# Two more steps before the normalizations of a routing batch, and the sigmoids of two batches in one place

## The chip, the core and the metric

The kernel runs on one core of a Trainium2 chip. The metric is device time in microseconds of one execution, given as the median of several runs. A profiled execution comes beside it; all durations below are from that one. Engines are named as in the profile: PE (TensorE), PEld (its weight loads), ACT (ScalarE), DVE (VectorE), POOL (GpSimd), SP (SyncE, which only issues DMAs).

## The reference, cut to what matters

The kernel computes a layer norm, then the sum of the input, a gated linear attention and a mixture of 64 experts, for 4 sequences of 2048 tokens with 256 features.

```python
xn = _layernorm(x)                                   # 8192 tokens x 256
# attention, 8 heads, keys of 128, values of 64, per token:
alpha = sigmoid((xn @ Wg + bg) / 16)                 # the decay of each head
state = alpha * state + k * v
out_t = einsum(q, state)
attn = (out * sigmoid(xn @ Wog)) @ Wo
# experts:
scores = sigmoid(xn @ gate_w.T)                      # 8192 x 64
# 4 of 8 groups by their two best scores + bias, then the 8 best experts of these;
# an expert takes its first 256 tokens
y = (silu(x_e @ w_gate) * (x_e @ w_up)) @ w_down     # added to the token, weighted by its scores
x = x + attn + moe
```

The decay `alpha` and the `scores` both come from one product of a token with 64 + 8 columns, and both go through a sigmoid.

## The kernel before

**Stages.** The tokens pass in 16 routing batches of 512 (`RB`, index `b`) and 32 attention blocks of 256 (index `s`). The attention blocks run one behind another over the whole kernel. Beside the first 16 of them run the fronts and backs of the routing batches, beside the later ones the experts.

**Steps.** The order of the work is written out in `block(s)`. A block has two halves; each takes the output products `od` of the half before, the state's update `dp`, then two projections of keys (`pj` with `wk`), two of queries (`wq`), transposes of keys (`kp`), the output projection (`wo`), values (`wv`) and gates (`wog`), and products of keys and queries (`sp`). Between these parts it calls `step()`, 12 times a block (`STEPS`). A step advances each generator in the list `side` whose start is due to its next `yield True`. Fronts of batches from 3 on start 12 steps apart, one per block: `start_front(b)` is `(b - 2) * STEPS`. `back(b)`, which picks the experts from the scores, starts at step `b * STEPS + 3`; `decays(i)` starts with the last batch of its group (`DGROUPS`: batches 0; 1; 2 and 3; 4 to 7; 8 to 11; 12 to 15).

**A front.** `front(b)` takes the statistics on DVE (L350 to L359); at the next step POOL works out the factors `rstd` and `nb` of the normalization in 14 small operations (L375 to L380) and SP loads the next batch's rows (`load_x`). Then come four steps, each with one ACT normalization of 128 tokens (L396), and after every second of these an ACT cast to fp16 (`x16`, L400) and a POOL subtraction for the low part (L401). The rows go to `xw_d` in DRAM (L404); `turn_tokens` transposes them on PE (`tp`, L340); the transposed tokens go to `xT_d` (L412). Last comes the product `lg` with the routing and decay columns, an addition of the bias on DVE (`zs`, L425), and two sigmoids on ACT: `sg` (L428, for the decays) and `sc` (L430, the scores).

**The decays.** `decays(i)` takes the logarithm of `sg` on ACT (L442), and later exponentials (L460, L462). The blocks use ACT for the high fp16 part of every projection (`split`, L229; DVE makes the low part from it, L230), for exponentials (L956) and for a tanh (L879). Sigmoid, Ln and Exp lie in different ACT tables; where a function is not in the table that is loaded, the compiler puts an `ACT_TABLE_LOAD` before it, which the profile shows under the line of that function.

**Order on an engine.** Each engine runs its instructions in order. A planner at build time chooses that order out of the program's order and its own times (`schedule_with_timeline_sim=True`); `tc.issue_after(x)` tells it to put instructions behind `x`. So an edit in one place can move instructions in others. PSUM tiles of the blocks come from a pool of four (`ps["pj"]`), those of routing and experts from a pool of two (`ps["mo"]`).

Of the kernel before, what the change touches and what calls it, by code (L numbers as in the profile page):

```python
# [13 lines left out]
AF = mybir.ActivationFunctionType  # L14
# [11 lines left out]
E, CAP, I = 64, 256, 128  # L26
# [39 lines left out]
def bc(ap, axis, n):  # L66

    a = ap.unsqueeze(axis)
    shape = list(a.shape)
    shape[axis] = n  # L70
    return a.to_broadcast(shape)
# [3 lines left out]
def gla_moe_kernel(ctx: ExitStack, tc: tile.TileContext, x, Wq, Wk, Wv, Wo, Wg, bg, Wog,  # L75
                   gate_wT, gate_bias, w_gate, w_up, w_down, out):
    nc = tc.nc
# [68 lines left out]
    made = {}  # L146
    WQ, WK, WV, WOG, GATE, WG = range(6)
# [5 lines left out]
    unfit = const.tile([P, 6], F32, name="unfit")  # L153
# [122 lines left out]
    def product(out_, a, b, first=True, last=True):  # L276

        nc.tensor.matmul(out_, lhsT=a[0], rhs=b[0], start=first, stop=False)  # L278
        nc.tensor.matmul(out_, lhsT=a[0], rhs=b[1], start=False, stop=False)  # L279
        return nc.tensor.matmul(out_, lhsT=a[1], rhs=b[0], start=False, stop=last).ins  # L280
# [40 lines left out]
    zs = r1.tile([P, NB, H, RT], F32, name="zs")  # L321
    sg = r1.tile([P, NB, H, RT], F32, name="sg")
    batch = {}

    def load_x(b):
        rows = slice(b * RB, (b + 1) * RB)
        xt = r2.tile([P, RT, D], F32, name="xt")
        src = xf[rows, :].rearrange("(t p) d -> p t d", p=P)
        n = 2 if b == 0 else RT
        for t in range(0, RT, n):  # L330
            nc.sync.dma_start(out=xt[:, t:t + n], in_=src[:, t:t + n])
        batch[b] = {"xt": xt}

    def turn_tokens(x16, xT):
        for t in range(0, RT, 2):
            tp = ps["mo"].tile([P, 2, 2, 2, P], F16, tag="mo", name="tp")
            for t2 in range(2):
                for a in range(2):
                    for c in range(2):
                        nc.tensor.transpose(tp[:, t2, a, c, :], x16[:, t + t2, a, c * P:(c + 1) * P], identh)  # L340
            nc.vector.tensor_copy(xT[:, t:t + 2], tp)

    def front(b):

        rows = slice(b * RB, (b + 1) * RB)
        xt = batch[b].pop("xt")
        st = r2.tile([P, RT, 6], F32, name="st")
        mv = r2.tile([P, RT, 2], F32, name="mv")
        for t in range(RT):
            nc.vector.bn_stats(out=st[:, t, :], in_=xt[:, t, :])  # L350
        for t in range(RT):
            nc.vector.bn_aggr(out=mv[:, t, :], in_=st[:, t, :])

        va = r2.tile([P, RT], F32, name="va")
        nc.vector.tensor_scalar(va, mv[:, :, 1], EPS, XFIT ** -2, ALU.add, ALU.mult)
        yi = r2.tile([P, RT], I32, name="yi")
        nc.vector.tensor_scalar(yi, va.bitcast(I32), 1, None, ALU.logical_shift_right)
        rstd = r2.tile([P, RT], F32, name="rstd")
        nc.vector.tensor_scalar(rstd.bitcast(I32), yi, -1.0, float(0x5f3759df), ALU.mult, ALU.add)  # L359
        yield True  # L360
        nt = r2.tile([P, RT], F32, name="nt")
        nb = r2.tile([P, RT], F32, name="nb")
        x16 = r1.tile([P, RT, 2, D], F16, name="x16")
        flat = x16.rearrange("p t a d -> p t (a d)")
        xT = r2.tile([P, RT, 2, 2, P], F16, name="xT")
        if b < 2:
            for _ in range(3):
                nc.vector.tensor_tensor(nt, rstd, rstd, ALU.mult)
                nc.vector.scalar_tensor_tensor(nt, in0=nt, scalar=-0.5, in1=va, op0=ALU.mult, op1=ALU.mult)
                nc.vector.scalar_tensor_tensor(rstd, in0=nt, scalar=1.5, in1=rstd, op0=ALU.add, op1=ALU.mult)  # L370
            nc.vector.scalar_tensor_tensor(nb, in0=mv[:, :, 0], scalar=-1.0, in1=rstd,
                                           op0=ALU.mult, op1=ALU.mult)
        else:
            for _ in range(3):
                nc.gpsimd.tensor_tensor(nt, rstd, rstd, ALU.mult)  # L375
                nc.gpsimd.tensor_tensor(nt, nt, va, ALU.mult)
                nc.gpsimd.tensor_scalar(nt, nt, -0.5, 1.5, ALU.mult, ALU.add)
                nc.gpsimd.tensor_tensor(rstd, rstd, nt, ALU.mult)
            nc.gpsimd.tensor_tensor(nb, mv[:, :, 0], rstd, ALU.mult)
            nc.gpsimd.tensor_scalar(nb, nb, -1.0, None, ALU.mult)  # L380
        if b < 2:
            for t in range(RT):
                made["hi"] = nc.scalar.activation(x16[:, t, 0, :], xt[:, t, :], AF.Identity,
                                                  bias=nb[:, t:t + 1], scale=rstd[:, t:t + 1]).ins
                xn = t5.tile([P, D], F32, tag="t5", name="xn")
                with tc.issue_after(made["xn"]) if b == 0 and t == 2 else ExitStack():
                    nc.vector.tensor_scalar(xn, xt[:, t, :], rstd[:, t:t + 1], nb[:, t:t + 1], ALU.mult, ALU.add)
                made["xn"] = nc.vector.tensor_tensor(x16[:, t, 1, :], xn, x16[:, t, 0, :], ALU.subtract).ins
        else:
            if b < NB - 1:  # L390
                load_x(b + 1)

            for t in range(RT + 1):
                yield True
                if t < RT:
                    nc.scalar.activation(xt[:, t, :], xt[:, t, :], AF.Identity,  # L396
                                         bias=nb[:, t:t + 1], scale=rstd[:, t:t + 1])
                if t in (2, 4):
                    ts = slice(t - 2, t)
                    nc.scalar.copy(x16[:, ts, 0, :], xt[:, ts])  # L400
                    nc.gpsimd.tensor_tensor(x16[:, ts, 1, :], xt[:, ts], x16[:, ts, 0, :], ALU.subtract)  # L401
        if b < 2:
            turn_tokens(x16, xT)
        made["xw"] = nc.sync.dma_start(out=xw_d[rows, 0:D].rearrange("(t p) d -> p t d", p=P),  # L404
                                       in_=flat.bitcast(F32)).ins
        yield True
        if b >= 2:
            if b > 2:
                yield True
            turn_tokens(x16, xT)  # L410
            yield True
        stored = nc.sync.dma_start(out=xT_d[b], in_=xT)  # L412
        with tc.issue_after(stored.ins):
            nc.sync.dma_start(out=of[rows, :], in_=xf[rows, :])
        batch[b]["xT"] = xT
        if b == 1:
            load_x(2)
        for _ in range(2 if b > 2 else 1):
            yield True
        lg = ps["mo"].tile([P, RT, E + H], F32, tag="mo", name="lg")  # L420
        for t in range(RT):
            for c in range(2):
                made["lg"] = product(lg[:, t, :], (xT[:, t, 0, c, :], xT[:, t, 1, c, :]),
                                     (gwz[:, 0, c, :], gwz[:, 1, c, :]), c == 0, c == 1)
        nc.vector.scalar_tensor_tensor(zs[:, b].rearrange("p h t -> p t h"), in0=lg[:, :, E:E + H],  # L425
                                       scalar=unfit[:, WG:WG + 1], in1=bc(brow, 1, RT),
                                       op0=ALU.mult, op1=ALU.add)
        nc.scalar.activation(sg[:, b], zs[:, b], AF.Sigmoid)  # L428
        sc = r3.tile([P, RT, E], F32, name="sc")
        nc.scalar.activation(sc, lg[:, :, 0:E], AF.Sigmoid, scale=unfit[:, GATE:GATE + 1])  # L430
        batch[b]["sc"] = sc
        yield True

    def decays(gi):
# [361 lines left out]
    side = []  # L796
# [381 lines left out]
    nc.vector.tensor_scalar(brow, brow, 1.0 / GATE_NORM, None, ALU.mult)  # L1178
    squares(WOG, raw["wog"][1][0][1])
    f0 = front(0)  # L1180
    for _ in range(3):
        next(f0)
# [70 lines left out]
    def start_front(b):  # L1253
        return 0 if b < 2 else 8 if b == 2 else (b - 2) * STEPS

    side.append((20, expert_fits(FITS[0])))
    for b in range(NB):
        if b:
            f = front(b)
            side.append((start_front(b), f))  # L1260
            if b == 1:
                with after(made["lo wk"]):
                    next(f)
        side.append((b * STEPS + (3 if b else 5), back(b)))
        for i, (b0, nb_) in enumerate(DGROUPS):
            if i and b0 + nb_ - 1 == b:
                side.append((start_front(b) + (12 if b > 2 else 6), decays(i)))

    unit_l(0, 0, 0)
    unit_a(0, 0, 0)  # L1270
# [54 lines left out]
```

## Time and profile before

| | |
|---|---|
| runs, median (lowest to highest) | 1272.43 us (1270.54 to 1278.66), 3 runs |
| the profiled execution | 1262.07 us |
| its span, first to last instruction | 1260.3 us |
| mean granted PE clock | 0.995 |
| busy: PE, PEld, DVE, ACT, POOL | 1188.0, 1018.4, 981.5, 914.0, 717.0 us |
| ACT table loads | 39, of 1283 ns each |
| normalizations on ACT (L396) | 56, mean 591 ns |

A group's row in the profile reads: line, engine, operation, output<-inputs, shape, count | busy time, mean of one in ns | idle time of the engine just before these instructions, and what ended it. A row of waits reads: who waited <- for what: total us, times, longest us. A row of the timeline reads: start in us, duration, engine, line, operation.

### The profile page before, as it was taken

The numbers are of one execution on the slowest core, as the hardware profiler recorded it, in microseconds if no ns is written. First come the engines' busy times: TensorE is split into PE (matmuls) and PEld (weight loads), VectorE is DVE, ScalarE is ACT, GpSimd is POOL, SyncE is SP. The second block draws the span as 40 slices with busy tenths as digits, with TensorE's granted clock in tenths as the row PEclk, the third lists the DMA queues.
The fourth block names the chain that finished last, engine by engine and source line by source line (L and its number), as shares of the span: only waits on it lengthen the run. The fifth ranks groups of instructions, "written<-read, shape, count | busy, mean of one in ns | idle before, by whom it ended". The sixth has DMA issues, their size and how long they took to land.

```text
span 1260.3 us, 35303 instructions
## 1 busy us (share of the span) xinstructions
PE 1188.0 (94%) x13799; PEld 1018.4 (81%) x13799; DVE 981.5 (78%) x2757; ACT 914.0 (73%) x1664; POOL 717.0 (57%) x899
## 2 busy tenths in 40 slices
PE   7799999999999998999799999999999999999997
PEld 6588777777888777788688888888888888888886
DVE  6988867686787876777778788878787878787864
ACT  5567676676767676666578898878888778778864
POOL 1476657765666566644335675626676757665330
PEclk9999999999999999999999999999999999999999
DMA  7446544535445554432657787768877777666531
GB/s 242 133 126 183 156 136 148 151 94 152 117 131 163 157 143 129 134 100 73 184 144 171 192 207 191 184 154 194 217 194 177 153 181 167 163 146 145 115 68 35
DMA packets 192615, 190.57 MB, mean 151 GB/s; under 512 B 35456, under 2 KB 163328, under 8 KB 191744
## 3 DMA queue, kind: packets, MB, share of 16 engines
q1 hardware_dynamic: 158928, 138.75, 36.2%
q0 software_dynamic: 29712, 45.89, 20.7%
q10 hardware_dynamic: 3808, 3.67, 0.8%
q8 instruction: 108, 1.77, 0.6%
q14 instruction: 59, 0.48, 0.1%
HBM read 141.14 MB, written 58.38 MB: 158 GB/s over the span
## 4 chain that ended last, share of the span: by engine, by line
PE 52%; DVE 19%; ACT 8%; POOL 8%; issue 6%; DMA 6%; SPq 2%; DVEq 0%; POOLq 0%; ACTq 0%
PE pj L278 8%; PE pj L280 8%; PE pj L279 8%; PE od L997 3%; PE od L1003 2%; PE kp L936 2%; DVE qt L912 2%; DVE ql L230 2%; PE xet L694 2%; PE gu L280 2%; PE gu L278 2%; PE gu L279 2%; DVE dc L981 2%; DMA el<-el_d 2%; POOL ol L1042 1%
## 5 line engine op out<-in xcount | busy, mean ns | idle before, releaser
L754 POOL DMA_INDIRECT out_dram<-y,idx x128 | 214.1, 1673 | 158.6 <-ACT y L740 50.8
L672 POOL DMA_INDIRECT xe<-xw_d,idx x128 | 137.5, 1074 | 40.3 <-issue 30.5
L278 PE MATMUL pj<-xs,wq_h 128*128 128x256 f16 x496 | 136.1, 274 | 8.2 <-DVE k L230 6.5
L230 DVE SCALAR_TENSOR_TENSOR k<-pj,k 128x512 f16<-128x512 f32 x128 | 87.0, 684 | 69.2 <-ACT k L229 68.3
L280 PE MATMUL pj<-xs,wq_l 128*128 128x256 f16 x496 | 136.2, 275 | 0.0
L279 PE MATMUL pj<-xs,wq_h 128*128 128x256 f16 x496 | 136.1, 274 | 0.0
L279 PE MATMUL pj<-xs,wk_h 128*128 128x256 f16 x496 | 135.2, 273 | 0.2 <-issue 0.2
L280 PE MATMUL pj<-xs,wk_l 128*128 128x256 f16 x496 | 135.2, 273 | 0.0
L278 PE MATMUL pj<-xs,wk_h 128*128 128x256 f16 x496 | 135.2, 273 | 0.0
L981 DVE TENSOR_TENSOR dc<-sp,dc 128x512 f32<-128x512 f32 x128 | 87.7, 685 | 46.4 <-POOL dc L961 25.5
L997 PE MATMUL od<-dc,v 128*64 128x128 f32 x1024 | 101.3, 279 | 4.5 <-DVE dc L981 4.5
L279 PE MATMUL sp<-ql,k 128*128 128x128 f16 x512 | 96.1, 219 | 7.8 <-DVE ql L230 6.9
L278 PE MATMUL sp<-qh,k 128*128 128x128 f16 x512 | 99.2, 220 | 4.3 <-ACT qh L229 2.2
L229 ACT ACTIVATE k<-pj 128x512 f16<-128x512 f32 x128 | 74.2, 591 | 33.6 <-PE pj L280 26.4
L280 PE MATMUL sp<-qh,k 128*128 128x128 f16 x512 | 96.0, 219 | 0.0
L229 ACT ACTIVATE qh<-pj 128x512 f16<-128x512 f32 x128 | 76.0, 596 | 25.8 <-PE pj L280 21.7
L1003 PE MATMUL od<-qt,state 128*64 128x128 f32 x960 | 94.7, 273 | 0.0
L1041 ACT CAST oh<-oT 128x512 fp32r<-128x512 f32 x64 | 39.6, 618 | 72.4 <-DVE oT L1011 68.6
L230 DVE SCALAR_TENSOR_TENSOR ql<-pj,qh 128x512 f16<-128x512 f32 x128 | 86.8, 679 | 4.4 <-ACT qh L229 4.1
L936 PE MATMUL kp<-identh,k 128*128 128x128 f16 x1024 | 82.5, 220 | 6.2 <-DVE k L230 3.4
L955 ACT ACTIVATE dc<-lp 128x512 f32<-128x512 f32 x128 | 76.3, 596 | 15.8 <-PE lp L951 14.3
L912 DVE SCALAR_TENSOR_TENSOR qt<-pj,el 128x512 f32<-128x512 f32 x128 | 86.8, 679 | 0.7 <-DMA el<-el_d 0.7
(421 smaller groups left out, 4512.0 us busy)
## 6 DMA issues: line engine op xcount, KB each, us to landing
el<-el_d SPq DMA_DIRECT2D x64, 512.0 KB
xw_d<-x SPq DMA_DIRECT2D x16, 512.0 KB
xT_d<-xT SPq DMA_DIRECT2D x16, 512.0 KB
out_dram<-in_L_attn_x_dram SPq DMA_DIRECT2D x16, 512.0 KB
nw<-in_L_ffn_w_gate_dram SPq DMA_DIRECT2D x64, 128.0 KB
nw<-in_L_ffn_w_up_dram SPq DMA_DIRECT2D x64, 128.0 KB
nw<-in_L_ffn_w_down_dram SPq DMA_DIRECT2D x64, 128.0 KB
w<-in_L_ffn_w_gate_dram SPq DMA_DIRECT2D x64, 128.0 KB
```

The costliest lines, as they stand in the source:

```text
L229: return (nc.scalar.activation(hi, t, AF.Copy, scale=scale).ins, nc.vector.scalar_tensor_tensor(lo, in0=t, scalar=scale, in1=hi, op0=ALU.m ...
L230: nc.vector.scalar_tensor_tensor(lo, in0=t, scalar=scale, in1=hi, op0=ALU.mult, op1=ALU.subtract).ins)
L278: nc.tensor.matmul(out_, lhsT=a[0], rhs=b[0], start=first, stop=False)
L279: nc.tensor.matmul(out_, lhsT=a[0], rhs=b[1], start=False, stop=False)
L280: return nc.tensor.matmul(out_, lhsT=a[1], rhs=b[0], start=False, stop=last).ins
L672: in_turn(lambda: nc.gpsimd.indirect_dma_start(out=xe[:, f, :], out_offset=None, in_=xw_d[:, :], in_offset=bass.IndirectOffsetOnAxis(ap=id ...
L754: two = [in_turn(lambda: nc.gpsimd.indirect_dma_start(out=of, out_offset=bass.IndirectOffsetOnAxis(ap=idx[:, e, f:f + 1], axis=0), in_=m[" ...
L912: read = nc.vector.scalar_tensor_tensor(qt, in0=pj, scalar=QFIT, in1=two_heads(el, i), op0=ALU.mult, op1=ALU.mult)
L936: nc.tensor.transpose(kp[:, i, :], k[:, i, :], identh)
L981: anchor.append(nc.vector.tensor_tensor(dc, B["sp"], dc, ALU.mult).ins)
L997: mm = nc.tensor.matmul(od[i * DV:(i + 1) * DV, n, j, :], lhsT=v[:, h0 + 2 * j + i, :], rhs=dc[:, 2 * j + i, :], start=True, stop=first)
L1003: mm = nc.tensor.matmul(od[i * DV:(i + 1) * DV, n, j, :], lhsT=state[half][:, 2 * j + i, :], rhs=qt[:, ck, 2 * j + i, :], start=False, sto ...
```

## The change

- For batches from 3 on, two more steps lie between the POOL factors and the first ACT normalization. All that follows in the front comes two steps later; `decays` starts two steps later as well. `load_x` and `back` keep their steps.
- For the even batches from 2 on, DVE copies the raw products into `sc`, and no sigmoid is taken. With the odd batch behind it, ACT takes `sg` of both batches in one instruction, then the sigmoid of the copied `sc` in place, then that of its own `sc`; `issue_after` keeps the three in this order.

```diff
@@ front(b), batches from 2 on
             if b < NB - 1:
                 load_x(b + 1)
+            if b > 2:
+                for _ in range(2):
+                    yield True
 
             for t in range(RT + 1):
                 yield True
...
-        nc.scalar.activation(sg[:, b], zs[:, b], AF.Sigmoid)
+
         sc = r3.tile([P, RT, E], F32, name="sc")
-        nc.scalar.activation(sc, lg[:, :, 0:E], AF.Sigmoid, scale=unfit[:, GATE:GATE + 1])
         batch[b]["sc"] = sc
+        if b > 1 and b % 2 == 0:
+            nc.vector.tensor_copy(sc, lg[:, :, 0:E])
+        else:
+            b0 = b if b < 2 else b - 1
+            made["sg"] = nc.scalar.activation(sg[:, b0:b + 1].rearrange("p b x y -> p (b x y)"),
+                                              zs[:, b0:b + 1].rearrange("p b x y -> p (b x y)"), AF.Sigmoid).ins
+
+            if b0 < b:
+                with tc.issue_after(made["sg"]):
+                    sc0 = batch[b0]["sc"]
+                    made["sg"] = nc.scalar.activation(sc0, sc0, AF.Sigmoid, scale=unfit[:, GATE:GATE + 1]).ins
+            with tc.issue_after(made["sg"]):
+                nc.scalar.activation(sc, lg[:, :, 0:E], AF.Sigmoid, scale=unfit[:, GATE:GATE + 1])
         yield True
...
-                side.append((start_front(b) + (12 if b > 2 else 6), decays(i)))
+                side.append((start_front(b) + (14 if b > 2 else 6), decays(i)))
```

## The prediction

> **What bounds the kernel now.** I read the page first (engine shares), then the stretches of the run, then TensorE's waits in the routing stretch, then ScalarE's groups there, and last one half-block in order of time.
>
> ```profile
> PE 1188.0 (94%) x13799; PEld 1018.4 (81%) x13799; DVE 981.5 (78%) x2757; ACT 914.0 (73%) x1664; POOL 717.0 (57%) x899
> ```
>
> TensorE (PE) is busy 94% of the span, and no other engine comes near. So the end moves only by what TensorE idles, and the change adds and removes no matmul. The stretches (columns: PE, PEld, DVE, ACT, POOL busy) say where it idles:
>
> ```profile
> 80.00:560.00 480.00, 448.54 (x5381) 378.99 (x5380) 360.04 (x1082) 331.97 (x614) 309.67 (x546) 0.99 0.48 140
> 650.00:1260.00 610.00, 595.96 (x6908) 519.76 (x6905) 489.58 (x1249) 480.57 (x872) 343.21 (x249) 1.00 0.69 161
> ```
>
> From 80 to 560 us the fronts of batches 3 to 15 run beside the attention blocks, and TensorE idles 480 - 448.5 = 31.5 us. The change touches this stretch alone: in the orders of the two built programs TensorE's sequence is the same again once the experts start. **31.5 us (2.5%) is the most that can come of it.** TensorE's own waits there (80 to 600 us; total, times, longest):
>
> ```profile
> PE tp L340 <- ACT x L400: 10.8, 10, 2.7
> PE pj L278 <- DVE k L230: 5.4, 7, 1.2
> PE sp L279 <- DVE ql L230: 4.4, 7, 1.5
> PE kp L936 <- DVE k L230: 2.8, 5, 1.3
> PE kp L936 <- ACT dc L955: 1.9, 2, 1.2
> ```
>
> The first is the change's target: the transposes of a batch's tokens stand still until ScalarE (ACT) has cast the normalized rows. The other four have ScalarE behind them too: VectorE's low parts `k` and `ql` wait for ScalarE's high parts (in this stretch VectorE waits 60.0 us for ScalarE's `k`). So TensorE idles where ScalarE runs late. ScalarE's groups show with what:
>
> ```profile
> L396 ACT ACTIVATE xt<-xt,nb,rstd 128x256 f32<-128x256 f32 x52 | 27.2, 591 | 6.8 <-POOL nb L380 6.8
> L428 ACT ACT_TABLE_LOAD x14 | 18.0, 1283 | 0.2
> L956 ACT ACT_TABLE_LOAD x13 | 16.7, 1283 | 0.2
> L430 ACT ACTIVATE sc<-lg,unfit 128x256 f32<-128x256 f32 x14 | 6.4, 456 | 0.0
> ```
>
> Each front loads the sigmoid table and, soon after, the exp table again. One half-block that starts its `od` products at 190.16:
>
> ```profile
> 194.44 0.62 ACT L1041 CAST oh<-oT 128x512 fp32r<-128x512 f32 x1 [2.60 <-DVE oT L1011]
> 194.96 0.59 ACT L955 ACTIVATE dc<-lp 128x512 f32<-128x512 f32 x1
> 195.57 1.28 ACT L956 ACT_TABLE_LOAD   x1
> 196.86 0.63 ACT L956 ACTIVATE dc<-dc 128x512 f32<-128x512 f32 x1
> 197.40 1.06 ACT L229 ACTIVATE k<-pj 128x512 f16<-128x512 f32 x2
> 198.35 0.60 ACT L955 ACTIVATE dc<-lp 128x512 f32<-128x512 f32 x1
> 198.95 2.08 ACT L396 ACTIVATE xt<-xt,nb,rstd 128x256 f32<-128x256 f32 x4
> ...
> 201.45 0.57 ACT L229 ACTIVATE qh<-pj 128x512 f16<-128x512 f32 x1
> ```
>
> The keys' first projection was done at 194.3, its cast starts at 197.4; a table load and four normalizations stand before `qh`. TensorE idles 0.79 us (for `k`), 0.29 (transposes) and 0.49 (`ql`), 1.6 us in all. Thirteen half-blocks hold normalizations; adding up TensorE's gaps of over 0.25 us in them gives about 27 us, so **2.1 us each**; some 4.5 us lie elsewhere.
>
> **The change, part by part.**
>
> *Two steps more before the normalizations (b > 2).* Nothing is added; normalizations, casts, transposes, the stores of `xw_d` and `xT_d`, logits and decays come two steps later, on SP's queue past the loads of half a block; `load_x(b + 1)` keeps its step. In the built order the casts keep about their place on ScalarE, but the transposes move back on TensorE. Batch 6: before, the casts stand behind the 19th and 20th `qh` and the transposes behind the 20th query projection; after, the casts stand the same and the transposes behind the 21st and 22nd. Batch 5: casts behind `qh` 14, transposes behind projection 15, becomes 16 and 18. That is about one half-block (480/27 = 17.8 us) of cover where there was none; in batches 9 and 11 it is the rest of the half-block. I take the 10.8 us of transposes as gone, with nothing late in their place: GpSimd's low part (1.23 us) follows the cast within the same cover. SP's stores have blocks of slack; the tightest, the decays of batches 2 and 3, are used a block after they are written.
>
> *Even batches from 2 on: a copy instead of two sigmoids.* Seven VectorE copies of 128x256 f32 out of PSUM. The trace has the same copy (L1031, `state<-dp`, 0.414 us): 7 x 0.414 = 2.9 us on an engine with 120 us idle in the stretch, so nothing; without that cover up to 2.9 us.
>
> *Odd batches: three sigmoids in one table.* The built program has 25 table loads, before 39: 14 fewer. The row gives 1.283 us, and the next instruction starts 1.30 after the load: 14 x 1.30 = 18.2 us less ScalarE time. [...] In this trace the load follows at 0.02 us behind the instruction before it and no drain shows, so I take 18. The sigmoid of the copied scores reads SBUF, which no sigmoid does here: between 0.456 us (L430, out of PSUM) and 0.591 (L396, SBUF, two pointer operands); I take 0.5, 3.5 us for seven, against seven `sg` of 0.23 saved. [...]
>
> *Half-blocks with sigmoids and normalizations together: six* (sigmoids of 3 to 13, normalizations of 4 to 14). Most read: `oh`, `dc`, `dc`, `k`, table, `sg`, `sc`, `sc` (with Ln: table, Ln), `k`, `dc`, table, `dc`, three normalizations, `qh`. With starts as in the trace, counted from `od`: `oh` +2.9 (the usual; 4.3 at 190.16), first `k` +5, table, sigmoids to +7.4, second `k` to +7.9 (its projection ends at about +6.5: covered), `dc` +8.4, table to +10.3, `dc` to +10.8, normalizations to +12.3, `qh` done +12.9, `ql` (0.68) +13.6. TensorE wants `ql` at about +11.5: 2.1 us idle. Check on the half-block at 190.16: `qh` ended at +11.9, `ql` +12.6; TensorE, already 1.1 late, waited 0.5. With Ln (batches 3, 7, 11) ScalarE has 1.6 us more: 3.7 us. The half-block at 117.5 held both tables, Ln and four normalizations, with `qh` at +12.6, and idled 1.7 us. I take 2.7. Six: 3 x 2.1 + 3 x 2.7 = 14.4 us, where 6 x 2.1 = 12.6 were: **+1.8 us**.
>
> *Half-blocks with normalizations and no table: seven.* First `k` at +5, `qh` at +8.6 behind the projection's end, then normalizations; transposes far off. About 0.3 us left each: 7 x (2.1 - 0.3) = **-12.6 us**. The sigmoids of batch 15 add 0.2.
>
> **Sum:** -12.6 + 1.8 + 0.2 = -10.6 us. Against the profiled execution (1262.1 us; span 1260.3) that is 1251.5. The profiled execution lies 10 us under the median of the runs shown (1272.4); the same difference from the median gives 1261.7, and I say **1261.7 us**, 0.8% less. About 1% is what a measurement of this kernel tells from no change.
>
> **Rivals.**
> 1. *ScalarE catches up everywhere.* The six table half-blocks become as quiet as the seven, since 18 us of loads are gone and the sigmoids fall where ScalarE waited for TensorE (12.7 us before `k`). Then 13 x 1.8 = 23.4 us: 1249. For: second `k` is covered. Against: the second load and three normalizations still stand before `qh`.
> 2. *The gain is given back.* While TensorE stood at the transposes, ScalarE and VectorE caught up; without that stop the next wait (`k`, `ql`, `od`) grows. If two thirds of 10.8 come back: -3.4, 1269. For: VectorE waits 60 us for `k`. Against: free half-blocks have ScalarE early.
> 3. *Slower: normalizations wait for GpSimd in front of `qh`.* In the table half-blocks GpSimd's addition `sfc` stands before the last factor, and `sfc` waits for the sigmoid. By my times it waits to +7.1, the last factor is ready at +8.4, normalizations start at +10.8: 2.4 us to spare. If GpSimd has a backlog (it is 65% busy here, and a normalization did wait up to 2.5 us for L380), `qh` and all after it go back by it: 2.5 us x 6 = 15, net +4.4: 1277. It turns the sign from 1.8 us a half-block on, and passes 1% from 3.9.
> That pairing doesn't do what it says is excluded: the built program has the 14 loads less.
>
> **How the numbers follow.** Forecast 0.52 (own range 1256 to 1268, half of it beyond 1%), rival 1 0.20 (nearly all beyond 1%), rival 2 0.14, rival 3 0.14 (over half beyond 1%). Faster 0.45, same 0.47, slower 0.08. The range runs from rival 1 to rival 3: 1249 to 1277.
>
> **What would show it.** Right: the row `tp L340 <- ACT x L400` nearly gone; TensorE idle from 80 to 550 us at about 21; VectorE's wait for `k` well below 60; 25 table loads; what remains sits in the half-blocks with sigmoids, as `sp <- ql`. Wrong: `xt <- POOL nb` grown with `qh` late behind it (rival 3), idle TensorE of 28 or more with `tp` gone (rival 2), under 14 (rival 1).

## The result and the profile after

The changed kernel takes **1280.59 us** (median of 15 runs, 1277.95 to 1285.82) against 1273.71 of the kernel before on the same chip (15 runs, 1269.14 to 1279.53). The ratio is **1.0056, 95% interval 1.0037 to 1.0075**: slower by 6.9 us, where 10.6 us less were forecast. The profiled execution took 1285.82 us with a span of 1284.1 and a mean TensorE clock of 0.988.

The two first profiles exaggerate: before's (1262.07) lies under all its other runs, after's at the top of its own. In the second profiles of the same two kernels, on one chip, the spans are 1268.6 and 1271.7, and that one of after is the fastest of its runs. So where several profiles of a kernel exist, a reading counts only if all of them have it.

The page's engine shares, after:

```profile
PE 1197.0 (93%) x13793; PEld 1023.7 (80%) x13799; DVE 991.1 (77%) x2764; ACT 897.9 (70%) x1643; POOL 714.8 (56%) x899
```

The routing stretch from 80 to 560 us (busy PE, PEld, DVE, ACT, POOL, then the granted clock):

```profile
80.00:560.00 480.00, 443.43 (x5273) 373.29 (x5273) 358.54 (x1050) 303.34 (x573) 301.48 (x535) 0.98 0.47 139
```

ScalarE lost 28.6 us of busy time here (331.97 before; 16.1 us over the whole run, since the slower kernel also gets less done in these 480 us), and TensorE idles **36.6 us, 5.1 more than before**. The clock column went from 0.99 to 0.98. TensorE's waits there, 80 to 600 us:

```profile
PE sp L279 <- DVE ql L230: 8.9, 13, 1.3
PE kp L951 <- DVE k L230: 5.4, 5, 1.5
PE ltp L500 <- DVE lt L488: 3.6, 1, 3.6
PE pj L278 <- DVE k L230: 3.4, 2, 2.1
PE od L1012 <- DVE dc L996: 3.2, 5, 1.3
PE sp L278 <- ACT qh L229: 3.0, 6, 1.2
```

The transposes' wait of 10.8 us is gone, as forecast. In its place `ql` doubled (4.4 to 8.9), the transposes of keys wait for `k` (2.8 to 5.4; the projections less, 5.4 to 3.4), `qh` itself is waited for, and the decays have one new stop of 3.6 us. What VectorE and ScalarE wait for says who is late. VectorE's waits in the same stretch, before:

```profile
DVE k L230 <- ACT k L229: 64.6, 32, 5.8
DVE dc L981 <- POOL dc L961: 25.5, 20, 3.7
```

and from VectorE's and from ScalarE's, after:

```profile
DVE dc L996 <- POOL dc L976: 33.4, 23, 4.0
DVE k L230 <- ACT k L229: 23.1, 27, 2.0
```

```profile
ACT xt L399 <- POOL nb L380: 20.9, 10, 3.9
```

VectorE waited 64.6 us for ScalarE's `k` before, and waits 23.1 now. But the normalizations' wait for GpSimd's last factor `nb` rose from 6.8 to 20.9. All profiles have both (`k`: 62.2 in the second of before, 20.4 and 23.2 in the other two of after; `nb`: 5.4, then 17.6 and 19.3). VectorE's wait for GpSimd's masked decays `dc` also rose in this pair, from 25.5 to 33.4, but not surely: the second profile of before has 27.7, the second of after 27.5. **ScalarE now waits for GpSimd where VectorE waited for ScalarE.** ScalarE's groups from 80 to 560 us:

```profile
L399 ACT ACTIVATE xt<-xt,nb,rstd 128x256 f32<-128x256 f32 x52 | 27.7, 589 | 20.9 <-POOL nb L380 20.9
L438 ACT ACT_TABLE_LOAD x6 | 7.7, 1283 | 0.1
L971 ACT ACT_TABLE_LOAD x6 | 7.7, 1283 | 0.1
L444 ACT ACTIVATE sc<-sc,unfit 128x256 f32<-128x256 f32 x6 | 3.0, 493 | 0.0
```

There are 6 + 6 table loads where 14 + 13 were (25 where 39 were in the whole run), at the same 1283 ns, and the sigmoid out of SBUF takes 0.493 us (0.5 was taken). The saving on ScalarE is as large as counted. TensorE gets nothing of it.

### A half-block without sigmoids

The forecast called the half-blocks with normalizations and no sigmoids quiet. One of them, in the second profile of the changed kernel, starts its `od` at 223.87. In order of time, ScalarE:

```profile
232.04 0.58 ACT L229 ACTIVATE qh<-pj 128x512 f16<-128x512 f32 x1
236.16 1.58 ACT L399 ACTIVATE xt<-xt,nb,rstd 128x256 f32<-128x256 f32 x3 [3.54 <-POOL nb L380]
237.65 0.57 ACT L229 ACTIVATE qh<-pj 128x512 f16<-128x512 f32 x1
```

and GpSimd, its first and its last operations on the factors:

```profile
226.57 0.38 POOL L375 TENSOR_TENSOR nt<-rstd 128x4 f32<-128x4 f32 x1
...
231.47 1.27 POOL L1057 TENSOR_TENSOR ol<-oT,oh 128x512 fp32r<-128x512 f32 x1
232.69 0.20 POOL L378 TENSOR_TENSOR rstd<-rstd,nt 128x4 f32<-128x4 f32 x1
...
235.29 0.64 POOL L976 TENSOR_SCALAR_AFFINE_SELECT dc<-dc 128x512 f32<-128x512 f32 x1
235.90 0.23 POOL L380 TENSOR_SCALAR nb<-nb 128x4 f32<-128x4 f32 x1
```

ScalarE was not behind with its work. It stood still for 3.54 us all the same, because three normalizations stand in its order in front of the second `qh`, and the 14 small factor operations are spread over 9.6 us between GpSimd's larger ones. The last factor comes 12.3 us after `od`; the second `qh` starts at +13.8. TensorE idles 2.5 us from this `od` to the next (0.58 and 0.51 for two `ql`, 0.37 for `qh`, 0.62 for a copy out of PSUM, and smaller ones), where 0.3 was forecast. The first 0.58 is not the normalizations' doing: that `qh` was cast by 232.6, but VectorE stood 2.38 us at `dc`, for GpSimd, before it made the `ql`.

### A half-block with sigmoids

The half-block whose `od` starts at 190.1, first profile after. VectorE, in order of time:

```profile
195.09 0.69 DVE L230 SCALAR_TENSOR_TENSOR k<-pj,k 128x512 f16<-128x512 f32 x1 [0.16 <-ACT k L229]
199.79 0.69 DVE L996 TENSOR_TENSOR dc<-sp,dc 128x512 f32<-128x512 f32 x1 [4.01 <-POOL dc L976]
200.40 0.68 DVE L230 SCALAR_TENSOR_TENSOR k<-pj,k 128x512 f16<-128x512 f32 x1
```

ScalarE had cast the second `k` by 197.9. Its low part starts at 200.4, since VectorE stood 4.01 us at `dc`, which waits for GpSimd, which was busy without a pause with factors, `ol` and the state until it reached `dc` at 199.12. TensorE waited 1.37 us for that `k` and later 1.34 for a `ql`, 3.2 us in all. So "second `k` covered", which was right for ScalarE, did not hold for VectorE behind it.

### The profile page after: what moved, and what is told of

The parts are those of the page before. It is cut to its first block, busy times and chain, and to the rows that moved or that the text cites. A ratio compares the mean times of both kernels' runs of the same rounds, so it can differ in the third digit from the quotient of the medians.

```text
span 1284.1 us, 35285 instructions
## 1 busy us (share of the span) xinstructions
PE 1197.0 (93%) x13793; PEld 1023.7 (80%) x13799; DVE 991.1 (77%) x2764; ACT 897.9 (70%) x1643; POOL 714.8 (56%) x899
## 4 chain that ended last, share of the span: by engine, by line
PE 52%; DVE 17%; POOL 10%; ACT 8%; DMA 7%; issue 5%; SPq 1%; another core or an unknown queue 0%; POOLq 0%; ACTq 0%; DVEq 0%
PE pj L278 8%; PE pj L280 8%; PE pj L279 8%; DMA el<-el_d 5%; PE od L1012 3%; PE od L1018 3%; DVE ql L230 2%; PE kp L951 2%; PE gu L280 2%; DVE qt L927 2%; PE gu L278 2%; PE gu L279 2%; PE xet L709 2%; POOL ol L1057 2%; DVE dc L996 2%
```

## The experiments

Each ratio is against the kernel before, run beside it on the same chip. The chips differ (the kernel before took about 1272 us on two and 1256 on two others), so medians of different chips are not compared.

One reading of the traces orders most of them: what stands around the four casts with which ScalarE feeds TensorE in a half-block. I write `k` and `q` for the casts of keys and queries, `n` for one normalization, `S` for a batch's or a pair's sigmoids with their table, each half-block starting at its `oh`. The commonest forms of the half-blocks with normalizations, and where the sigmoids stand, 80 to 600 us:

```
kernel            normalizations                  S between the two k   ratio
before            kknnnnqq 6, nnnnkkqq 3          0 of 14               1
e_before_behind   kknqnqnn 8, kkqnnqnn 2          0 of 14               0.989
e_pairs_behind    kknqnqnn 5, kkqnnqnn 5          0 of 7                0.992
e_behind          kkqqnnnn 8, kSkqqnnnn 5         6 of 7                0.997
e_pairs           nnnnkkqq 6, kknnnnqq 4          0 of 7                1.005
after             kknnnnqq 3, kSknnnnqq 2,        5 of 7                1.006
                  kSknnnqnq 2, kkqnnnqn 2
e_unpaired        kSkqqnnnn 11                    12 of 14              1.007
e_steps           kSknnnnqq 6                     9 of 14               1.020
```

### The two halves of the change, and both kernels again

`e_steps`: the changed kernel with the old sigmoids.

```diff
-        if b > 1 and b % 2 == 0:
-            nc.vector.tensor_copy(sc, lg[:, :, 0:E])
-        else:
...
+        nc.scalar.activation(sg[:, b], zs[:, b], AF.Sigmoid)
+        nc.scalar.activation(sc, lg[:, :, 0:E], AF.Sigmoid, scale=unfit[:, GATE:GATE + 1])
```

> Only the two steps (and the decays two steps later); each batch keeps its own sigmoids. Theory S (the steps cost the time: transposes of the decays and the normalizations now stand in TensorE's and ScalarE's way elsewhere): ratio 1.003 to 1.008, the wait of the transposes for the casts gone, and a wait of some 3 us of the decays' transposes (ltp) as in the changed kernel. Theory P (the pairing costs it: two table loads and three sigmoids between the two casts of the keys): ratio 0.992 to 1.000 here.

Measured: **1.0196 (1.0162 to 1.0230)**, 1300.07 us. The steps are the costly half, far beyond the 1.003 to 1.008 that was expected of them. TensorE's waits, 80 to 560 us:

```profile
PE kp L939 <- DVE k L230: 9.7, 6, 2.7
PE sp L278 <- ACT qh L229: 8.5, 5, 2.3
PE sp L279 <- DVE ql L230: 6.2, 10, 1.3
```

ScalarE in one half-block, in order of time:

```profile
237.89 0.58 ACT L229 ACTIVATE k<-pj 128x512 f16<-128x512 f32 x1
238.49 1.28 ACT L431 ACT_TABLE_LOAD   x1
...
243.15 2.08 ACT L399 ACTIVATE xt<-xt,nb,rstd 128x256 f32<-128x256 f32 x4 [1.80 <-POOL nb L380]
245.25 1.28 ACT L959 ACT_TABLE_LOAD   x1
```

Before, all 14 sigmoids came at the end of a half-block, behind its four casts. Two steps later 9 of them start in the next half-block, between its two `k`, and in 7 of these 9 half-blocks normalizations stand as well. In the one shown TensorE waits 1.71 us for the second `k`, which is behind the sigmoids, and 1.88 for the first `qh`, which is behind four normalizations and the second table load. Nothing was added to the program; work was moved from where nobody waits to where TensorE does.

`e_pairs`: the changed kernel without the steps.

```diff
-            if b > 2:
-                for _ in range(2):
-                    yield True
...
-                side.append((start_front(b) + (14 if b > 2 else 6), decays(i)))
+                side.append((start_front(b) + (12 if b > 2 else 6), decays(i)))
```

> Only the pairing of the sigmoids; the steps as before. Theory S: ratio 0.985 to 0.998 (14 table loads of 1.3 us less in front of the casts of keys and queries), the wait of the transposes for the casts still 5 to 11 us. Theory P: ratio 1.003 to 1.008, with the time lost in the half-blocks that hold the sigmoids.

Measured: **1.0047 (1.0022 to 1.0073)**, 1281.29 us. With half the sigmoids' table loads gone and nothing moved to a later step, the kernel is no faster, rather slower. The transposes wait as before (80 to 560 us):

```profile
PE tp L340 <- ACT x L400: 10.1, 6, 3.0
```

The order on ScalarE shifted: four normalizations stand in front of both `k` in 6 half-blocks where it was 3, and they wait 14.6 us for `nb` (before: 6.8). That these two facts make the loss is my reading; the run by itself shows only that the loads saved are worth nothing here.

The effects do not add: +2.0% and +0.5% alone, +0.6 to +0.8% together. The pairing pays for most of what the steps spoil; it brings the half-blocks with sigmoids between the two `k` from 9 down to 5.

`e_after` and `e_before` are the two kernels unchanged.

> The changed kernel again, for a second profile: which of its waits come again (the 3.6 us before ltp, the 22 us of normalizations waiting for GpSimd's factors), and how many half-clock stretches of TensorE it has. If the clock makes the loss (theory C), its mean granted clock is below that of the kernel before by 0.004 to 0.008 in all its runs; if not, the clocks agree within 0.002. Ratio 1.004 to 1.008.

> The kernel before again, for a second profile and its clocks run by run. Ratio 0.998 to 1.002. The first profile was 10 us under the median of its runs: theory C expects this one nearer to 1273 us, with more half-clock stretches than four.

Measured: `e_after` **1.0067 (1.0042 to 1.0092)**, `e_before` **0.9989 (0.9969 to 1.0008)**. A third time, on another chip, `e_after_2`:

> The changed kernel once more, beside these two: ratio 1.004 to 1.009 if its loss is the same on this chip as in the sets of runs before.

Measured: **1.0082 (1.0058 to 1.0105)**. The loss is there each time; the difference of the first pair of profiles (23.8 us) is not. The mean granted clock was 0.987 over the runs of each of the two and 0.990 in the kernel before beside them: 0.003 lower, between the two cases that were named ahead of `e_after`.

### Normalizations behind the queries

`e_behind`: the changed kernel, with each normalization put behind the last query cast of the program so far.

```diff
-                    nc.scalar.activation(xt[:, t, :], xt[:, t, :], AF.Identity,
-                                         bias=nb[:, t:t + 1], scale=rstd[:, t:t + 1])
+                    with tc.issue_after(made["qh"]):
+                        nc.scalar.activation(xt[:, t, :], xt[:, t, :], AF.Identity,
+                                             bias=nb[:, t:t + 1], scale=rstd[:, t:t + 1])
```

> The changed kernel with one edit: the planner must put the normalizations behind the second query cast of the same half-block. Theory N (what the changed kernel loses beside its gain is that normalizations wait for GpSimd's factors in front of a query cast): the waits of TensorE for ql and qh fall from 11 to under 5 us, TensorE idles 5 to 8 us less in the routing stretch, ratio to the kernel before 0.995 to 1.001. Rival V (it is the volume of ScalarE's work in that half-block, wherever it stands): the waits only move to the casts behind (kt, values), ratio 1.003 to 1.008 as in the changed kernel.

Measured: **0.9967 (0.9950 to 0.9983)**, 1252.68 us against 1256.23. A half-block with normalizations reads `kkqqnnnn` or `kSkqqnnnn` now, and the wait for `ql` shrank from 8.9 to 0.7 us. The waits, 80 to 560 us:

```profile
PE ltp L501 <- DVE lt L489: 7.7, 3, 2.8
PE pj L278 <- DVE kt L960: 4.7, 5, 1.3
...
PE sp L279 <- DVE ql L230: 0.7, 2, 0.3
```

With the same steps and the same pairs, and only the normalizations no longer in front of the queries, the loss becomes a gain of 0.3%. Against the changed kernel on other chips (1.0056 to 1.0082) that is 0.9 to 1.1%. This is the order that the forecast had assumed, and what normalizations in front of the queries cost the changed kernel. Whether they also make it slower than before is another question: the kernel before has them there too, and `e_before_behind` below bears on it.

`e_ltp`: the changed kernel, with the decays' transposes three steps later, against the new stop of 3.6 us.

```diff
         made["lt2"] = nc.vector.tensor_copy(lt[:, :, :, 2, :], r4).ins
         yield True
+        if gi > 1:
+            for _ in range(3):
+                yield True
```

> The changed kernel with three more steps between the low parts of the decays (lt) and their transposes (ltp), for the groups from batch 2 on. If the single wait of 3.6 us before ltp (and the half-clock stretch behind it) is a part of the loss: that wait gone, ratio 1.002 to 1.005. If another wait takes its place: 1.005 to 1.009.

Measured: **1.0062 (1.0040 to 1.0084)**. No gain. The stop is gone, and another stands in its place (80 to 560 us):

```profile
PE sp L279 <- DVE ql L230: 7.2, 11, 1.2
PE kp L954 <- ACT dc L973: 7.1, 3, 5.0
```

`e_both` has both edits.

> Both edits, normalizations behind the second query cast and ltp three steps later. Theory N: ratio 0.990 to 0.998, TensorE idle in the routing stretch under 28 us, half-clock stretches no more than before. Rival V: 1.000 to 1.006.

Measured: **0.9940 (0.9920 to 0.9961)**, 1247.61 us, against 0.9967 of `e_behind`; the intervals overlap a little. Against `e_ltp` (1263.87 us) it differs by the normalizations' place alone, on the same chip: 1.3% less, and no run of the one overlaps with any of the other. With the queries free, the `ltp` wait of 7.7 us was the largest, and moving it away may bring some 0.3%.

`e_dve`: the changed kernel, the factors of all batches on VectorE instead of GpSimd (the form of the first two batches).

```diff
-                nc.gpsimd.tensor_tensor(nt, rstd, rstd, ALU.mult)
-                ...
-            nc.gpsimd.tensor_scalar(nb, nb, -1.0, None, ALU.mult)
+                nc.vector.tensor_tensor(nt, rstd, rstd, ALU.mult)
+                ...
+            nc.vector.scalar_tensor_tensor(nb, in0=mv[:, :, 0], scalar=-1.0, in1=rstd,
+                                           op0=ALU.mult, op1=ALU.mult)
```

> The changed kernel with the factors of all batches worked out on VectorE (10 small operations of some 0.2 us in place of 14 on GpSimd). Theory N: the wait of normalizations for the factors (18 to 21 us) gone, ratio 0.995 to 1.002. But the planner then puts the normalizations elsewhere, some in front of key casts, beside the table loads; if that decides (rival V), ratio 1.005 to 1.015 with the factors' wait gone all the same.

Measured: **1.0184 (1.0162 to 1.0206)**. A miss. ScalarE's waits and TensorE's, 80 to 560 us:

```profile
ACT xt L398 <- DVE nb L378: 21.0, 12, 3.9
```

```profile
PE pj L278 <- DVE k L230: 15.5, 8, 3.8
PE kp L950 <- ACT dc L969: 9.3, 4, 3.0
```

The normalizations wait as long as in the changed kernel, for another engine. Bursts of four normalizations stand in front of the first `k` in three half-blocks (one in the changed kernel), perhaps because the planner takes the factors as ready earlier; ScalarE waits there, and the keys behind it. It did take load off GpSimd: VectorE's wait for `dc` fell to 17.4 us. So moving the factors to another engine doesn't help by itself: ScalarE's order still has, in front of a cast that TensorE needs, something whose input is late (21.0 us of waiting).

### Which of the parts is worth something in a good order

`e_unpaired`: steps and the `issue_after`, without the pairing.

> The two steps and normalizations behind the second query cast, but each batch keeps its own sigmoids: what the pairing is worth in the arrangement in which normalizations are out of the way. The table loads then stand between the two key casts in every block instead of every second one. Theory N with the table half-blocks as costed (some 2 to 3 us each, seven more of them): ratio 1.005 to 1.012, against 0.9967 with pairs. If table loads cost nothing once normalizations are out of the way: 0.994 to 1.000.

Measured: **1.0069 (1.0044 to 1.0094)**. The sigmoids stand between the two `k` in 12 of 14 half-blocks, and the second `k` is late (80 to 560 us):

```profile
PE kp L940 <- DVE k L230: 12.1, 8, 3.3
```

Against `e_behind` (0.9967, on another chip) the pairing is worth 1.0% here: the forecast's reason for it is right, where a table load stands between casts.

`e_before_behind`: the kernel before with the `issue_after` alone (the diff of `e_behind`).

> The kernel before with the normalizations put behind the last query cast that the program has issued by then; without the two steps that is the one of the half-block before, so the planner still puts one or two of them in front of a query cast. Theory N: little is gained, ratio 0.994 to 1.002; the transposes' wait for the casts stays (8 to 13 us), as it has no half-block of cover. If the steps are not needed for the gain: under 0.994.

Measured: **0.9891 (0.9863 to 0.9920)**, 1258.42 us against 1271.93: the lowest ratio of all, and faster than both kernels. I had expected little, since the transposes were to wait as before. They don't. ScalarE in the half-block of the same batch, in order of time:

```profile
234.22 0.58 ACT L229 ACTIVATE qh<-pj 128x512 f16<-128x512 f32 x1
234.70 1.08 ACT L397 ACTIVATE xt<-xt,nb,rstd 128x256 f32<-128x256 f32 x2
235.69 0.58 ACT L229 ACTIVATE qh<-pj 128x512 f16<-128x512 f32 x1
236.16 0.59 ACT L397 ACTIVATE xt<-xt,nb,rstd 128x256 f32<-128x256 f32 x1
```

One or two normalizations stand between two casts instead of four in front of them, and the sigmoids stay at the end of the half-block. TensorE's waits and its stretch, 80 to 560 us:

```profile
PE pj L278 <- DVE k L230: 4.9, 9, 1.2
PE od L998 <- DVE dc L982: 2.6, 6, 0.8
PE sp L279 <- DVE ql L230: 2.4, 6, 0.7
```

```profile
80.00:560.00 480.00, 459.58 (x5529) 387.13 (x5527) 379.00 (x1110) 337.03 (x626) 314.82 (x552) 1.00 0.49 144
```

The idle time fell to 20.4 us, near the 21 that the forecast expected of the change, but by another edit, and with ScalarE the busiest of all versions (337.0). GpSimd's `dc` costs VectorE 12.4 us there, and of the normalizations' wait for `nb` (10.2 us) 6.2 stand in front of a cast of keys or queries, where in after 18.2 of 20.9 do.

`e_pairs_behind`: that version with the pairing.

> Pairs of sigmoids without the two steps, and the normalizations held back as in the run that took this edit alone (0.989): sigmoids then stand at the end of the half-block before, and half of the blocks have no table load. If 14 table loads less are worth ScalarE's 18 us where nothing else stands in the way: ratio 0.978 to 0.986. If table loads at that place are hidden anyway: 0.986 to 0.993. If the batch of three sigmoids and its tables is worse than two of two: over 0.993.

Measured: **0.9920 (0.9893 to 0.9947)**, 1248.36 us against 1256.47. In this order the pairing adds nothing: `e_before_behind` has the same ratio within the intervals. The table loads stand behind the last cast of a half-block there, and to save them saved nothing that could be measured.

Side by side, the eight versions show three edits, each with and without the others:

```
                     the planner's order     normalizations behind the queries
before               1                       0.989
pairs                1.005                   0.992
steps                1.020                   1.007
steps and pairs      1.006, 1.007, 1.008     0.997
```

To put the normalizations behind the queries brings 0.9 to 1.3% in every row, in the kernel before as much as in the changed one. So their place explains why the hoped-for gain did not come. Whether it also makes the changed kernel slower than before stays open: ScalarE's wait for `nb` in front of casts did grow (1.1 us in before, 15.2 to 18.2 in the profiles of after, none in `e_behind`), but with the normalizations behind the queries the change still costs as much (0.997 against 0.989). The steps alone cost 2.0%, and still 1.8% with the normalizations mostly out of the way (1281.36 against 1258.42 us, on one chip). The pairing gives back 1.0 to 1.4% with the steps, and nothing without them. Both fit sigmoids between the keys' casts, which only the versions with steps have. But the steps move the casts, the transposes and the decays too, and no version kept the steps and held the sigmoids alone behind the query casts. That the sigmoids' place makes most of the loss is argued from these rows and not shown singly.

### A ledger with the clock

Over 29 half-blocks of the routing stretch, from one `od` to the same `od` in every kernel, I took from the trace the time, TensorE's idle time, and the time for which the granted clock was 0.5 (us):

```
                  time    idle   half clock   time - idle - half/2
before            514.0   32.0      6.8          478.6
e_before          517.5   33.0     13.7          477.7
after             525.4   38.1     17.1          478.8
e_after           521.7   36.5     13.7          478.4
e_after_2         526.6   40.0     17.1          478.1
e_steps           545.1   52.3     34.1          475.8
e_pairs           527.6   41.1     17.1          478.0
e_behind          511.2   28.7     10.2          477.4
e_both            506.7   28.5      3.4          476.5
e_before_behind   501.6   20.4      0.0          481.2
```

The last column varies by 5.4 us (475.8 to 481.2) while the times spread over 43 us; the four kernels not listed lie within it. So idle time, plus half of the time at half clock, is nearly the whole difference between these kernels. From before (mean of two profiles) to after (of three), the idle time grows by 5.7 us and the half-clock time by 5.7, which costs 2.9: 8.6 us in this stretch, where the medians differ by 6.9. The behaviour of the clock is shown at the end.

The same idle time, by what the half-block holds (number of half-blocks: us):

```
                 normalizations,  normalizations    no
                 no sigmoids      and sigmoids      normalizations
before           10: 20.6         3:  2.4           16:  8.9
e_before         10: 20.5         3:  2.2           16: 10.3
after             9: 21.0         4: 10.4           16:  6.7
e_after           9: 19.1         4: 10.8           16:  6.6
e_after_2         9: 20.2         4: 11.9           16:  7.9
e_behind          8:  5.9         5:  9.5           16: 13.2
e_before_behind  12: 16.7         2:  1.4           15:  2.4
```

The first column is what was to become quiet, and it stayed as it was, at 2.1 to 2.3 us each. In `e_behind`, with the normalizations really behind the queries, it fell to 0.7 each; there a part came back in the half-blocks without normalizations, whose idle time went from about 7 to 13.2 us. In the first two columns together the idle time grew, from before to after, from 22.9 us (mean of two) to 31.1 (of three); in the third it fell by 2.5. What sigmoids between the keys' casts cost is seen best in `e_behind`, where the normalizations of all thirteen stand behind the queries: 1.9 us each with such sigmoids, 0.7 without.

Behind the routing stretch the change does nothing that these profiles show. From the start of the experts' half-blocks on (26 of them), five versions on the two faster chips take 534.6 to 534.7 us each, `e_ltp` with all of the change as well as `e_pairs_behind`; on the others that stretch scatters between 540 and 548, whatever the version.

## Why the prediction was wrong, point by point

1. **The bound: right.** The change acts through TensorE's idle time in the routing stretch, and the ledger closes on it within some 5 us, with the clock as a second term that the prediction didn't have.
2. **Two steps more, the transposes' wait gone: right. "With nothing late in their place": wrong.** The row went from 10.8 us to none of note. But the steps move the sigmoids too, and these lost their cover: 0 of 14 between the keys' casts before, 9 of 14 with the steps alone. The prediction had the sigmoids in the half-blocks with normalizations in the built order, priced them with ScalarE's durations, and did not ask what they had cost at their old place. There, behind the last cast, eleven half-blocks with sigmoids and no normalizations idled 0.3 us each, and `e_pairs` and `e_pairs_behind` gained nothing by halving them.
3. **Fourteen loads, 18.2 us: right as a count, wrong as a gain.** ScalarE's busy time fell by 16.1 us over the run, and the loads that are left take 1283 ns each, with 0.1 us of idle time in all before each row of six. Alone it gave 1.0047, and in the good order nothing; it is worth 1.0% only where the loads stand between casts (`e_unpaired` against `e_behind`). Here the place decided, and not the 1283 ns of a load.
4. **Half-blocks with normalizations and sigmoids, 2.1 to 2.7 us each, +1.8 us: near as an amount, wrong as a difference.** The trace has four and not six (the sigmoids of batches 9 and 11 stand at the end of half-blocks without normalizations), at 2.6 to 3.0 us each. In the one shown, the second `k`, called covered, cost 1.37 us (1.15 in the second profile), since VectorE's low part of it stands behind `dc` and GpSimd. But the sum took off, for what these half-blocks had idled before, a mean of 2.1 us over all thirteen with normalizations. In the trace of before that mean hides two kinds: ten with normalizations in front of a cast, and no sigmoids, idled 2.1 each, and three with sigmoids, both behind the queries, only 0.8 (23.0 us together, where the prediction read about 27). The thirteen idle 8.3 us more after the change, where the sum had 10.8 less.
5. **Half-blocks with normalizations and no table, 0.3 us each, -12.6 us: this is the step that failed.** The prediction had normalizations behind the queries, with ScalarE early. The trace has nine such half-blocks and not seven; in eight of them two or more normalizations stand in front of a query cast, and ScalarE, early indeed, waits for GpSimd's `nb` (17.6 to 20.9 us over all thirteen). They idle 2.1 to 2.3 us each, 19.1 to 21.0 in sum, as before: none of the 12.6 came. Nine times about 1.9 us more than forecast is about 17; the forecast of the idle time in the profile (20.9) missed by 15.7. `e_behind` is the test: in the order that was assumed, such half-blocks idle 0.7 each.
6. **Rival 2 had its sign, and was given 14%: 28 us or more of idle time with the transposes' wait gone.** The wait for `ql` did grow as it said (4.4 to 8.9 us), that for `k` hardly in sum (8.2 to 8.8). That the gain must be given back is not so: in `e_before_behind` the transposes' wait is gone as well, and the idle time fell by 11 us.
7. **Rival 3 had the mechanism, in the wrong place and too small.** It put the wait for `nb` in front of `qh`, but into the half-blocks with tables, with the last factor at +8.4. The measured +12.3 in a free half-block is 3.9 later, because GpSimd's factor operations don't run in one go. Its sign in the list was right: "`xt <- POOL nb` grown with `qh` late behind it". It was given 14%. That its +4.4 us lay near the measured +6.9 is luck in part, since it is 2.5 us for each of six half-blocks with tables, and the wait for `nb` in the one shown was 0.81.
8. **Not in the sum: the clock and the decays.** Half-clock periods cost 2.9 us more in the ledger's stretch; the decays' later start brought one stop of 3.6 us, seen in all three profiles. `e_ltp` shows that to remove this stop alone gains nothing (another took its place), so it isn't the cause by itself.

What stays open: why the planner puts normalizations ahead of the factors they need (its own times were not compared with the trace operation by operation), and how much GpSimd's `dc` alone costs. To run the 14 factor operations in one go, ahead of `ol` and the state, was not tried, nor was the good order together with an earlier `dc`, nor the sigmoids alone behind the query casts with the steps kept.

## What to carry to other kernels

When a change relieves the engine that is late, look up which engine it waits for next, and when that one delivers in this stretch, operation by operation: here ScalarE lost 16 us of work and stood still for GpSimd instead. Before you move work by some steps, ask what it costs where it is, and take no mean over unlike places: sigmoids at the end of a half-block cost nothing that could be measured, and between the casts of the keys, in `e_behind`, 1.2 us each time. An edit of the order on the one engine that feeds the bound (a normalization behind a query cast) was worth 0.9 to 1.3%, more than all the work taken away.

## What the runs showed of the hardware

From 80 to 600 us the granted TensorE clock was 0.50 in before for two stretches of 3.41 us (from 165.07 and 308.43 us), and in after for three of 3.41 us (from 130.22, 205.31 and 536.40 us) and one of 6.83 us (from 287.23 us); in the rest it was 1.00. Within each of the two traces, the starts of all half-clock stretches of the run lie whole multiples of 3.413 us apart (the four of before 37, 42 and 94 times that), so these traces can be cut into such periods. Four periods of after, 201.87 to 208.70 and 532.96 to 539.79 us (busy PE, PEld, DVE, ACT, POOL, then the clock):

```profile
201.87:205.29 3.42, 1.75 (x16) 1.34 (x14) 3.28 (x15) 3.42 (x7) 1.07 (x2) 1.00 0.00 0
205.29:208.70 3.41, 3.22 (x13) 1.58 (x14) 1.91 (x5) 1.93 (x6) 3.41 (x4) 0.50 0.35 95
532.96:536.37 3.41, 1.51 (x16) 0.88 (x14) 3.19 (x16) 3.41 (x9) 0.60 (x2) 1.00 0.33 92
536.37:539.79 3.42, 3.39 (x18) 2.35 (x18) 1.52 (x3) 1.33 (x3) 3.42 (x5) 0.50 0.81 207
```

In the first, TensorE was busy 1.75 us of 3.42, with no single wait over 1.34 us; the next period ran at 0.50. From 80 to 600 us, the first profiles of before and after have some 300 such periods, and eight of these at full clock were busy 51% or less. Six of the eight were followed by half clock, two (45 and 49% busy) were not, and no busier one at full clock was. The share busy alone does not tell the two from the six (33 to 51% busy); what decides is not shown. The ledger counts half of a period at half clock as lost, 1.7 us. That is an estimate, from the products of queries in before (`pj <- xs,wq`, 128x256), which start 0.11 us apart at 164.5 us and 0.21 us apart at 165.5. Whether the same short waits, far apart, would have cost less was not tested by any run.
